# A 7x7 convolution for attention over 49 shifts: rows in polynomial form, column pairs by three products, the input kept on chip

## The chip, the cores and the metric

The kernel runs on one core of a Trainium2 chip. Its engines are TensorE (PE; its weight loads are listed apart as PEld), VectorE (DVE), ScalarE (ACT), GpSimd (POOL) and SyncE (SP). Each works through its own queue in order and waits on semaphores; SP's queue, and here and there ScalarE's, issue the DMA transfers. Everything is fp32. The metric is device time in microseconds (us), lower is better.

## The reference

Two layers, on x of shape (4, 256, 64, 64). Layer 0 makes 49 weights for every pixel and adds up 49 shifted copies of x with them. Layer 1 is a bottleneck block whose three normalisations use the batch's own statistics.

```python
# layer 0
k = conv(x, w1, pad=6, rhs_dilation=2) + b1        # w1: (128, 256, 7, 7)
k = conv(k, w2) + b2                               # w2: (49, 128, 1, 1)
attn = softmax(k, axis=1)                          # over the 49
shifts = stack([xp[:, :, 2*u:2*u+64, 2*v:2*v+64] for u in range(7) for v in range(7)], axis=1)
x = einsum('bkchw,bkhw->bchw', shifts, attn)       # xp: x padded by 6
# layer 1
h = relu(bn(conv(x, w1, 1x1)))                     # 256 -> 64
h = relu(bn(conv(h, w2, 3x3, pad=1)))              # 64 -> 64
out = relu(bn(conv(h, w3, 1x1)) + x)               # 64 -> 256
```

## The kernel before

No nonlinear step lies between the first two convolutions, so the kernel multiplies w1 by w2 first (`product`, line 332) and runs one 7x7 convolution from 256 channels to 49 values. As taps are two apart, rows and columns of different parity never meet: an image falls apart into four of 32 x 32, and pixels are ordered by column, image, parities and row tile.

**Rows.** Four output rows of a column need ten input rows. They are computed by evaluating at ten points: 0, infinity, and plus and minus 0.4, 0.8, 1.25 and 2.5. `product` evaluates the weights there. VectorE evaluates x: `combine` makes sums over rows by chains of `scalar_tensor_tensor` (line 150), `mix` makes the values at +p and -p from the even and odd parts, and `apply_factor` divides a factor out of the stored rows between passes. A pass is one pair of points.

**Columns.** `column_convs` (line 262) takes one column of 128 channels x 128 pixels as the stationary operand, in two halves of 64 (`HALVES`), and streams the weights of its 7 column taps, up to 7 x 49 = 343 columns, into PSUM banks that hold strips of eight output columns. Each matmul of the code shows as two records in the profile. There are 32 columns, ten points and two halves of the 256 channels.

**Order.** All five passes run for channel half 0 first. After each strip ScalarE copies the sums out of PSUM and sends them to DRAM (`put_aside`). Meanwhile half 1 of x is sorted into `stage` and kept in DRAM (`ready`, `fsort`). Then the passes run again for half 1: `put_back` brings the sums to PSUM, and `outputs` adds each pass, scaled, into the logits of four rows. Up to there TensorE's and VectorE's order is the program's (`manual_schedule`); in the second half only SP's first part is fixed and a planner orders the rest.

**Behind it.** For a strip of eight columns `exponents` subtracts the maximum (VectorE) and takes Exp (ScalarE); `shares` divides by the sum and writes the 49 weights into one of three padded rows (`pads`). `turn` transposes a half strip with 8 transposes for each of four output rows (line 568), and ScalarE, or ScalarE and VectorE where it is called with `shared`, copies the result into `amat` (lines 575, 573). `gather` (line 768) multiplies x by `amat`: that is the sum over the 49 shifts. The bottleneck follows (lines 801 to 1091).

The lines that matter here:

```python
for s in range(2 * h, 2 * h + 2):                  # L493, passes 1 to 4, half 0
    column_convs(s, u, True)
    put_aside(n, s)
...
if p is None and 0 < s < NS - 1:                   # L660, last pass, half 1
    if s == 2:
        turn(0, 0)
    exponents(s - 1)
    shares(s - 1)
```

Of the kernel before, what the change touches and what calls it, by code (L numbers as in the profile page):

```python
# [64 lines left out]
PIECES = ((0, 16), (16, 24), (40, 24))  # L65
READY = ((0, 1), (1, 4), (4, NT))
HALVES = (slice(0, 64), slice(64, 128))
ROWS2 = 16
NS, WS = 4, 8
KV = K7 * K  # L70
# [5 lines left out]
NR = 19  # L76
CW = 16
RW = R * CW
AT = 2 * (R // 4) * 4 * 2 * 64 * 4
XI = 2 * R * B * Q * NR  # L80
UT = XI + 2 * R * B * Q * NT
ARENA = UT + NH * (2 + 2 * NP) * KV
SW = WS * CW


def _poly(squares):

    c = [1.0]
    for s in squares:
        c = [(c[i - 1] if i else 0.0) - s * (c[i] if i < len(c) else 0.0) for i in range(len(c) + 1)]  # L90
    return c
# [3 lines left out]
def conv_seq_kernel(ctx: ExitStack, tc: tile.TileContext, xp, xt, w1, b1, w2t, b2, m1t, g1, be1,  # L95
                    m2t, g2, be2, m3t, g3, be3, z, mask, pavg, out, ydram):
    nc = tc.nc
    def pool(stack, name, bufs, space=None, **kw):
        if space is not None:
            kw["space"] = space  # L100
        return stack.enter_context(tc.tile_pool(name=name, bufs=bufs, **kw))


    keep = pool(ctx, "keep", 1)
    st1 = keep.tile([P, 2 * NT, 6], F32, name="st1")


# [18 lines left out]


    ready = nc.dram_tensor("ready_dram", (P, NS, 2, SW, NT), F32, kind="Internal").ap()
    fsort = nc.dram_tensor("fsort_dram", (P, 2, 2, RW // 2, NR), F32, kind="Internal").ap()
    aside = nc.dram_tensor("aside_dram", (1 + len(PAIRS), 2, NS, P, WS * K), F32, kind="Internal").ap()  # L130


    arena = pool(ctx, "arenap", 1).tile([P, ARENA], F32, name="arena")
    slots = arena[:, :XI].rearrange("p (k x i) -> p k x i", k=2, i=NR)
    xi = arena[:, XI:UT].rearrange("p (k x t) -> p k x t", k=2, t=NT)

    ut = arena[:, UT:].rearrange("p (h n v) -> p h n v", h=NH, v=KV)

    amat = arena[:, :AT].rearrange("p (g x c m e) -> p g x c m e", g=2, x=R // 2, c=2, e=4)
    XT = NT * C  # L140
    xts = {}

    units = [(b + 2 * g, 2 * a + c) for b in range(2) for g in range(2) for c in range(2) for a in range(2)]

    cst = pool(ctx, "cst", 1)
    w2sb = cst.tile([P, K], F32, name="w2sb")
    b1sb = cst.tile([P, 1], F32, name="b1sb")
    bias = cst.tile([P, K], F32, name="bias")
# [3 lines left out]
    def zero_rows(t):  # L152

        for k, i0, i1 in ((0, 0, 2), (1, 0, 1), (0, NR - 1, NR), (1, NR - 2, NR)):
            nc.gpsimd.memset(t[:, k, :, i0:i1], 0.0)

    zero_rows(slots)

    def sort_x(raw, b, r0, n, dst, w0, last=None, first=None):

        d = dst.rearrange("p k (w b e) i -> p k w b e i", b=B, e=Q)
        nw = d.shape[2]
        for k in range(2):
            m = r0 // 2 + (r0 // 2 + 3 + k) % 2
            count = ((r0 + n) // 2 - m + 1) // 2
            i = (m + 3) // 2
            for a in range(2):
                lo = 2 * m + a - r0
                (last if last and k + a == 2 else first if first and k + a == 0 else nc.scalar.copy)(  # L169
                    d[:, k, :, PLACE[b], 2 * a : 2 * a + 2, i : i + count],  # L170
                    raw[:, lo : lo + 4 * count - 3 : 4, PAD + 2 * w0 : PAD + 2 * w0 + 2 * nw].rearrange(
                        "p r (w c) -> p w c r", c=2
                    ),
                )

    squares = [p * p for p in PAIRS]
    d_zero = 1.0
    for s in squares:
        d_zero *= -s

    passes = [
        (PAIRS[0], None, squares),
        (PAIRS[1], squares[0], squares[1:]),
        (PAIRS[2], squares[1], squares[2:]),
        (PAIRS[3], None, squares[2:]),
        (None, None, squares[2:]),
    ]

    def combine(dst, row, first, coef):

        n = len(coef) - 1
        acc = row(first + 2 * n)
        for i in range(n - 1, -1, -1):
            stt(dst, row(first + 2 * i), coef[i], acc)
            acc = dst

    def even(p, left, row, x0):
        combine(x0, row, 2, _poly([q for q in left if q != p * p]))

    def odd(p, left, row, x1):  # L200
        combine(x1, row, 1, _poly([q for q in left if q != p * p]))

    def mix(p, x0, x1):
        stt(x0, x1, p, x0)
        stt(x1, x1, -2.0 * p, x0)

    def transform(p, left, row, x0, x1):
        if p is None:
            combine(x0, row, 0, _poly(left))
            combine(x1, row, 1, _poly(left))  # L210
            return
        even(p, left, row, x0)
        odd(p, left, row, x1)
        mix(p, x0, x1)

    def rows_of(t, cols=slice(None), tiles=(0, NT)):


        def row(n):
            i = n // 2 + 2 * tiles[0]  # L220
            return t[:, n % 2, cols, i : i + 2 * (tiles[1] - tiles[0]) - 1 : 2]

        return row

    def apply_factor(t, factor, n, cols=slice(None), parities=range(2)):

        for k in parities:
            v = t[:, k, cols, :n]
            stt(v, v, -factor, t[:, k, cols, 1 : n + 1])

    def visit(t, cols, p, left):

        transform(p, left, rows_of(t, cols), xi[:, 0, cols], xi[:, 1, cols])

    def strip(s, n=1):
        return slice(SW * s, SW * (s + n))

    def weights(n, half):

        return (ut[:, half, 1 + n, :], ut[:, half, 1 + NP + n, :]) if n < NP else (ut[:, half, 0, :], ut[:, half, 1 + 2 * NP, :])  # L240

    s_acc = ExitStack()
    accall = pool(s_acc, "accp", 1, PSUM).tile([P, 2 * NS, 512], F32, name="acc")
    acc = [[accall[:, 2 * s + i] for s in range(NS)] for i in range(2)]

    def strip_taps(s, w):

        return max(0, WS * s - w + 3), min(K7, WS * s + WS - w + 3)

    def column_convs(s, u, first):  # L250

        for d in (s - 1, s, s + 1):
            if not 0 <= d < NS:
                continue
            for i in range(2):
                for w in range(WS * s, WS * s + WS):
                    lo, hi = strip_taps(d, w)
                    if lo >= hi:
                        continue
                    o = (w - 3 + lo - WS * d) * K  # L260
                    for part in HALVES:
                        nc.tensor.matmul(  # L262
                            acc[i][d][part, o : o + (hi - lo) * K],
                            xi[:, i, CW * w : CW * w + CW, :].rearrange("p x t -> p (x t)")[:, part],
                            u[i][:, lo * K : hi * K],
                            start=(first and w == max(0, WS * d - 3)),
# [8 lines left out]
    with ExitStack() as s1:  # L275
# [13 lines left out]
        with ExitStack() as s2:  # L289
# [13 lines left out]
            for i, p in enumerate(PAIRS):  # L303
                nc.gpsimd.memset(points[:, i : i + 1], p)
# [844 lines left out]
```

## Time and profile before

| | |
|---|---|
| three runs | 775.61, 776.87 (median), 781.44 us |
| span of the profiled execution | 774.0 us |
| TensorE busy | 698.9 us, 7428 matmul records |
| VectorE busy | 580.0 us, 681 instructions |
| ScalarE, GpSimd busy | 305.2, 93.4 us |
| line 262 (column products) | 4000 records, 365.0 us |
| line 150 on `arena` (row points) | 192 instructions, 296.0 us |
| mean granted TensorE clock | 0.968 |
| DMA | 150.68 MB, mean 195 GB/s |

A run's time holds the span, from the first to the last instruction, and a little around it. Busy time is the union of an engine's instructions; matmuls are pipelined, so a record's duration is longer than its share of the stream. The granted clock is the part of full speed that TensorE was given. In lists, "out<-in" are tiles by their names in the code, "x80" counts instructions, and "<-" names what ended the idle time before.

### The profile page before, as it was taken

To read this page: it belongs to the slowest core of one execution; us is meant where nothing else is said; L and a number is where in the kernel's file an instruction comes from. 1 tells how busy PE (TensorE), PEld (TensorE's weight loads), DVE (VectorE), ACT (ScalarE), POOL (GpSimd) and SP (SyncE) were. 2 spreads that over 40 slices of the span, in tenths; PEclk is the share of its full clock that TensorE was granted. 3 is DMA by queue.
4 is the path that set the end of the run, shared out by engine and by line. 5 is a ranking of instruction groups with operands and counts; after the bars stand their busy time and mean duration, and the time that the engine had idled before them with its cause. 6 is when DMAs were issued, how large, how long until landed. Compare 5 with 4: busy or idle time off the path is not lost.

```text
span 774.0 us, 17422 instructions
## 1 busy us (share of the span) xinstructions
PE 698.9 (90%) x7428; PEld 506.4 (65%) x7428; DVE 580.0 (75%) x681; ACT 305.2 (39%) x600; POOL 93.4 (12%) x171
## 2 busy tenths in 40 slices
PE   1949898999998987999999999999989988998996
PEld 1937776666766654667666678988778863436642
DVE  5899899999839989999999967222232247854797
ACT  4517465112641011111112258433343346346497
POOL 3516100001000020000002213222212201000000
PEclk9979999999999998999999999999999998997997
DMA  8831299713998895111111013566676659144299
GB/s 348 341 161 43 71 323 344 302 42 138 311 351 320 316 378 174 53 43 44 43 42 33 3 58 105 188 237 226 219 233 232 231 188 406 36 156 174 102 391 377
DMA packets 59839, 150.68 MB, mean 195 GB/s; under 512 B 7410, under 2 KB 35698, under 8 KB 56178
## 3 DMA queue, kind: packets, MB, share of 16 engines
q1 hardware_dynamic: 53712, 141.51, 50.7%
q10 hardware_dynamic: 6050, 8.06, 2.9%
q8 instruction: 58, 0.95, 0.5%
q14 instruction: 19, 0.16, 0.1%
HBM read 93.81 MB, written 55.74 MB: 193 GB/s over the span
## 4 chain that ended last, share of the span: by engine, by line
PE 42%; DVE 33%; DMA 10%; issue 6%; ACT 6%; SPq 1%; ACTq 0%; POOL 0%; DVEq 0%
DVE arena L150 20%; PE acc L262 14%; PE acc L768 12%; DMA raw<-in_xp_dram 6%; PE pconv L975 4%; DVE arena L1084 3%; PE acc L801 3%; PE pdirect L963 3%; DVE stage_x L150 3%; PE acc L568 2%; DMA fsort_dram<-stage 2%; DVE outer L150 2%; PE moments L1045 1%; PE pturn L1040 1%; ACT arena L575 1%
## 5 line engine op out<-in xcount | busy, mean ns | idle before, releaser
L262 PE MATMUL acc<-arena 128*64 128x196 f32 (+6 forms) x4000 | 365.0, 345 | 27.4 <-DVE arena L150 13.2
L262 PEld LDWEIGHTS acc<-arena 128*64 128x64 f32 x4000 | 255.3, 138 | 136.3 <-issue 26.8
L150 DVE SCALAR_TENSOR_TENSOR arena<-arena 128x1024 f32<-128x1024 f32 (+7 forms) x192 | 296.0, 1585 | 9.5 <-ACT arena L169 3.6
L768 PE MATMUL acc<-arena,outer 128*64 128x128 f32 x2048 | 115.2, 273 | 9.0 <-issue 6.9
L768 PEld LDWEIGHTS acc<-arena,outer 128*64 128x64 f32 x2048 | 112.7, 137 | 14.5 <-issue 12.7
L809 DVE BATCH_NORM_STATS2 st<-acc 128x6 f32<-128x512 f32 x16 | 11.1, 694 | 68.8 <-PE acc L801 68.8
L122 ACT COPY outer<-outer 64x2048 f32<-64x2048 f32 x15 | 28.5, 1899 | 76.9 <-DMA outer<-in_xt_dram 76.9
L169 ACT COPY stage<-raw 128x128 f32<-128x128 f32 x128 | 44.6, 419 | 28.6 <-DMA raw<-in_xp_dram 23.8
L609 ACT COPY acc<-bks 128x392 f32<-128x392 f32 x40 | 18.6, 488 | 81.2 <-DVE outer L594 53.2
L286 ACT COPY sv<-acc 128x392 f32<-128x392 f32 x40 | 19.2, 485 | 75.2 <-PE acc L262 57.3
L1026 PE MATMUL pconv<-arena,w3m 64*128 64x512 f32 (+1 forms) x144 | 43.4, 591 | 0.6 <-DVE arena L1084 0.6
L150 DVE SCALAR_TENSOR_TENSOR outer<-outer 128x784 f32<-128x784 f32 (+2 forms) x47 | 36.9, 844 | 4.0 <-POOL outer L930 4.0
L123 POOL COPY outer<-outer 64x1792 f32<-64x1792 f32 x15 | 25.1, 1676 | 91.3 <-DMA outer<-in_xt_dram 91.3
L1026 PEld LDWEIGHTS pconv<-arena,w3m 64*128 64x128 f32 x144 | 20.9, 186 | 21.9 <-DVE arena L1084 16.1
L1089 ACT ACTIVATE outer<-arena 128x512 f32<-128x512 f32 (+1 forms) x58 | 34.6, 694 | 1.1 <-DVE arena L865 1.1
L1084 DVE SCALAR_TENSOR_TENSOR arena<-pconv,arena 128x512 f32<-128x512 f32 (+1 forms) x58 | 34.3, 670 | 0.0
L575 ACT COPY arena<-acc 128x512 f32<-128x512 f32 x52 | 27.1, 708 | 14.8 <-PE acc L568 14.4
L169 POOL COPY arena<-raw 128x192 f32<-128x192 f32 (+2 forms) x24 | 27.2, 1158 | 38.6 <-DVE arena L150 32.6
L975 PE MATMUL pconv<-outer,arena 128*128 128x512 f32 x72 | 31.1, 592 | 0.0
L592 ACT COPY outer<-acc 128x784 f32<-128x784 f32 x8 | 6.5, 813 | 59.7 <-PE acc L262 59.7
L789 DVE COPY bks<-acc 128x256 f32<-128x256 f32 x32 | 11.3, 418 | 24.8 <-PE acc L768 24.8
L169 ACT COPY arena<-raw 128x192 f32<-128x192 f32 (+2 forms) x36 | 20.6, 648 | 22.0 <-DVE arena L150 21.0
(149 smaller groups left out, 668.4 us busy)
## 6 DMA issues: line engine op xcount, KB each, us to landing
raw<-in_xp_dram SPq DMA_DIRECT2D x36, 608.0 KB, 5.5
outer<-in_xt_dram SPq DMA_DIRECT2D x17, 896.0 KB, 6.7
out_dram<-outer SPq DMA_DIRECT2D x14, 1024.0 KB, 4.5
arena<-y_dram SPq DMA_DIRECT2D x25, 512.0 KB, 8.2
fsort_dram<-stage SPq DMA_DIRECT2D x2, 4864.0 KB, 15.3
arena<-fsort_dram SPq DMA_DIRECT2D x8, 1216.0 KB, 8.4
y_dram<-outer SPq DMA_DIRECT2D x16, 512.0 KB, 4.6
aside_dram<-sv ACTq DMA_DIRECT2D x40, 196.0 KB, 5.5
```

The source lines that it names most:

```text
L122: nc.scalar.copy(t[:MID], x[MID:])
L123: nc.gpsimd.tensor_copy(t[MID:, : NT - 1], x[:MID, 1:])
L150: nc.vector.scalar_tensor_tensor(out, in0, scalar, in1, ALU.mult, ALU.add)
L169: (last if last and k + a == 2 else first if first and k + a == 0 else nc.scalar.copy)(d[:, k, :, PLACE[b], 2 * a : 2 * a + 2, i : i + count],
L262: nc.tensor.matmul(acc[i][d][part, o : o + (hi - lo) * K], xi[:, i, CW * w : CW * w + CW, :].rearrange("p x t -> p (x t)")[:, part], u[i][ ...
L575: nc.scalar.copy(dst, src)
L768: nc.tensor.matmul(dst[part, :: NT - 1] if edge else pts[c][part, o : o + 128], x[:, i, half * P + part.start : half * P + part.stop], ama ...
L801: nc.tensor.matmul(pt[a * MID : (a + 1) * MID, :], w1m[:, n, :], ys[a, n][:, 512 * i : 512 * i + 512], start=(n == 0), stop=(n == NH - 1), ...
L975: nc.tensor.matmul(m[k], wu[:, k, j, :], vs[k][:, g, j : j + R, :], start=(j == 0), stop=(j == 1))
L1026: nc.tensor.matmul(pt[:, :n], w3m[part, half * P : (half + 1) * P], h2[part, slot, q, lo : lo + n], start=True, stop=True)
L1084: nc.vector.scalar_tensor_tensor(v, conv3(b, q, i, half, lo, n), sc3[:, half : half + 1], v, ALU.mult, ALU.add)
L1089: nc.scalar.activation(dst, v.rearrange("p (r w) -> p r w", w=R), AF.Relu, bias=sh3[:, half : half + 1])
```

## The change

The row transform is turned round. x is sorted once into four planes, the rows 0 to 3 of each tile of four, for all 256 channels, and stays on chip. The four rows are the coefficients of a polynomial of degree 3, so its values at +p and -p take two sums and two mixing instructions (`even_part`, `odd_part`, `mix_plus`, `mix_minus`). The product of that polynomial with the weights' polynomial has ten coefficients; overlapping neighbours are added. Both steps, from points to rows and between tiles, are matmuls with 128 x 128 matrices made on the host (`_mats`, `final`).

Columns go in pairs, even and odd. Three streams replace two times seven taps: even columns with the 4 even taps, odd columns with the 3 odd taps, and their sums (`add_columns`) with the summed taps (4). `join_streams` subtracts the first two from the third and adds what belongs together.

Both channel halves of a pass now run one after the other into the same PSUM banks, so nothing is put aside; weights at the points are kept in DRAM (`wts`) and loaded pass by pass. A pass has two chunks of eight column pairs (c = 0, 1), a chunk four pieces (two halves of channels, two groups of four pairs). The pass for the points 0 and infinity is split: channel half 0 first, before half 1 has been read, with its sums kept in DRAM (`early`), half 1 last. All five engines follow the program's order.

```diff
-    def visit(t, cols, p, left):
-        transform(p, left, rows_of(t, cols), xi[:, 0, cols], xi[:, 1, cols])
...
-    def column_convs(s, u, first):
...
-        def put_aside(n, s):
...
-        def stage_rows(h):
...
-    def outputs(n, p, g):
...
-    def put_back(n, d):
...
+    def load_weights(n, half, slot):
+        w = wbuf[slot]
+        i = slice(0, 2 + 2 * NP, 1 + 2 * NP) if n == ZERO else slice(1 + n, 2 + n + NP, NP)
+        nc.sync.dma_start(out=w[:, :, :TAPS], in_=wts[half, :, i])
+        nc.gpsimd.tensor_tensor(w[:, :, 7 * K : 10 * K], w[:, :, : 3 * K], w[:, :, 4 * K : 7 * K], ALU.add)
+        nc.gpsimd.tensor_copy(w[:, :, 10 * K :], w[:, :, 3 * K : 4 * K])
...
+    def sort_x():
+        raw, half, b, r0 = queued.pop(0)
...
+        by = (nc.scalar.copy, nc.vector.tensor_copy, nc.gpsimd.tensor_copy)
+        for k, who in enumerate((0, 1, 2, 0, 1, 2, 0, 1)):
...
+    def even_part(m, cols):
...
+        nc.vector.scalar_tensor_tensor(main_of(m)[:, 0], x[:, SLOT[2]], p * p, x[:, SLOT[0]], ALU.mult, ALU.add)
...
+    def add_columns(q):
+        v = planes(q)
+        for i in range(2):
+            nc.vector.tensor_tensor(sums_of(q)[:, i], v[:, i, :, 0], v[:, i, :, 1], ALU.add)
+
+    def bank(cn, k):
+        return accall[:, (6 * cn + k) % 8]
...
+    def conv_group(q, st, i):
...
+        for k in range(4):
+            a = a0 + k
+            lo, hi = max(a, base), min(a + (4, 3, 4)[st] - 1, top)
+            x = sums_of(q)[:, i, k] if st == 2 else planes(q)[:, i, k, st]
+            for part in HALVES:
+                nc.tensor.matmul(
+                    pt[part, (lo - base) * K : (hi + 1 - base) * K],
+                    x[:, part],
+                    w[:, (lo - a) * K : (hi + 1 - a) * K],
...
+    def take_plus(cn, st):
...
+        nc.vector.tensor_tensor(s, pt, d, ALU.add)
+        nc.vector.tensor_tensor(d, pt, d, ALU.subtract)
+
+    def join_streams(cn):
...
+        nc.vector.tensor_tensor(t[:, :, :z], t[:, :, :z], t[:, :, 10 * K : 10 * K + z], ALU.subtract)
+        nc.vector.tensor_tensor(t[:, :, : 9 * K], t[:, :, : 9 * K], t[:, :, 20 * K :], ALU.subtract)
+        nc.vector.tensor_tensor(t[:, :, 11 * K : 20 * K], t[:, :, 11 * K : 20 * K], t[:, :, 20 * K :], ALU.add)
...
+        if last:
+            nc.vector.tensor_tensor(t[:, :, :CA], t[:, :, :CA], helds[c], ALU.add)
...
+    def final(task, pt, add=True):
...
+            nc.tensor.matmul(
+                pt[half, o : o + z], mats[:, r, half], ca, start=(one is None), stop=True, skip_group_check=True
+            )
...
+            nc.vector.tensor_tensor(dst, pt[:, :z], dst, ALU.add)
...
+    def run(tasks, cn, count, first=4, banks=2):
+        for _ in range(count):
+            if tasks:
+                n_final[0] += 1
+                final(tasks.pop(0), bank(cn, first + n_final[0] % banks))
...
+        for q, (cn, h, sub) in enumerate(pieces):
...
+            add_columns(q)
+            for do in pending:
+                do()
+            pending = []
+            if make:
...
+                even_part(m, cols)
+                odd_part(m, cols)
...
+                if len(halves) == 2 and in_chunk in (1, 2):
+                    share = len(waiting) if in_chunk == 2 else (len(waiting) + 1) // 2
+                    counts = {g: share * g // 5 - share * (g - 1) // 5 for g in range(1, 6)}
...
+            for g in range(6):
+                conv_group(q, g // 2, g % 2)
+                if make and g == 1:
+                    mix_plus(m)
+                if make and g == 3:
+                    mix_minus(m)
+                if g in counts:
+                    run(waiting, cn - 1, counts[g])
+                if ends and g in (1, 3):
+                    take_minus(cn, g // 2)
+                    take_plus(cn, g // 2)
+            if ends:
+                take_minus(cn, 2)
+                pending += [lambda cn=cn: take_plus(cn, 2), lambda cn=cn: join_streams(cn)]
...
+            if is_last and c == 1 and in_chunk == 1:
+                exponents(0)
+                shares(0)
+        cn = len(chunks) - 1
+        turn(0, 0)
+        turn(0, 1)
+        for do in pending:
+            do()
+        waiting = finals(cn)
+        for s in range(1, NS):
+            run(waiting, cn, 4, 6, 8)
+            exponents(s)
+            if s == 1:
+                shares(1)
...
-        turn(0, 1)
         zero_edges(0)
-        load_xt(xtiles[0], *units[0])
-        exponents(2)
         turn(1, 0)
-        exponents(3)
-        shares(2)
         turn(1, 1)
         zero_edges(1)
+        load_xt(xtiles[0], *units[0])
+        shares(2)
         turn(2, 0)
+        turn(2, 1, True)
+        zero_edges(2)
         shares(3)
         load_xt(xtiles[1], *units[0], 1)
-        turn(2, 1, True)
-        zero_edges(2)
         turn(3, 0, True)
         turn(3, 1, True)
         zero_edges(3)
```

A piece is made ready two pieces ahead (m = q - 2 in the count of the pair passes): its values at +p and -p lie in one of three buffers (`mains`). The column sums have one buffer. The finals of a chunk run in the second and third piece of the next; two PSUM banks are left to them.

## The prediction

> **What bounds the kernel now.** I read the page's busy times and slices first, then the groups by shape, then stages in the timeline.
>
> ```profile
> PE 698.9 (90%) x7428; PEld 506.4 (65%) x7428; DVE 580.0 (75%) x681; ACT 305.2 (39%) x600; POOL 93.4 (12%) x171
> ...
> PE   1949898999998987999999999999989988998996
> ...
> DVE  5899899999839989999999967222232247854797
> ```
>
> Up to slice 24 (some 460 us) TensorE and VectorE are both full; that is the 7x7 stage. Behind it TensorE alone is full, and the change leaves that part's code alone. Two rows fix the stage and the tail behind it:
>
> ```profile
> 48.53 19.83 PE L262 MATMUL acc<-arena 128*64 128x196 f32 x200 [11.13 <-DVE arena L349]
> ...
> 450.90 5.67 PE L262 MATMUL acc<-arena 128*64 128x343 f32 x46
> ...
> 468.28 10.03 ACT L575 COPY arena<-acc 128x512 f32<-128x512 f32 x20
> ...
> 484.75 15.50 PE L768 MATMUL acc<-arena,outer 128*64 128x128 f32 x280
> ```
>
> Column products run from 48.5 to 456.6 (408.1 us); the gather of layer 0 starts at 484.8, 28.2 us later. I forecast the new time of that gather; what follows it (774.0 - 484.8 = 289.2 us) stays.
>
> **TensorE, by columns streamed.** The dense stretch of the old products, each engine's busy time:
>
> ```profile
> 380.00:440.00 60.00, 60.00 (x676) 40.59 (x674) 1.00 0.09 25
> ```
>
> By shape these 676 records stream 141,022 columns in 60 us: 0.4255 ns a column. Each fp32 matmul of the code shows as two records. The old products stream 640x1078 + 480x294 = 831,040 columns: 353.6 us. The new ones: 11 tap blocks of 49 for a column pair instead of 14; 16 pairs give 176 blocks, of which 8 fall off the edges; 168 x 49 x 2 column halves x 2 records x 20 (ten points, two channel halves) = 658,560 columns, 280.2 us, or 7.0 us for each of 40 pieces. New are the 128x128 matrices (`final`): 1,568 columns x 4 rows x 2 x 2 x 5 passes = 125,440, 53.4 us. So TensorE sheds only 20 us of 354.
>
> One rule reads this otherwise. The Trainium skill, "Trainium Kernel Development and Optimization", Best Practices, judges TensorE by MFU and LDWEIGHTS busy share, not by matmul busy time. Weight loads go from 4,000 to 3,840 + 560, so by the load share the line-262 loads of 255.3 us would become 281, a loss of 26 us in place of the gain of 20. Here loads are busy 40.59 of 60 us while columns pass without a gap, so I go by columns.
>
> **VectorE.** Rows for its price:
>
> ```profile
> L150 DVE SCALAR_TENSOR_TENSOR arena<-arena 128x1024 f32<-128x1024 f32 x80 | 95.5, 1248 | 2.3 <-DMA arena<-ready_dram 2.0
> ...
> L593 DVE TENSOR_TENSOR outer<-acc,outer 128x784 f32<-128x784 f32 x8 | 7.8, 976 | 1.0 <-PE acc L262 1.0
> ...
> L349 DVE TENSOR_TENSOR arena<-arena,acc 128x196 f32<-128x196 f32 x14 | 5.0, 359 | 0.5
> ```
>
> 95.5/80 = 1.19 us for 1024 elements. Between 196 and 784 the slope is 1.05 ns an element; back to back four 784s take 3.54 us, so a queued instruction costs about 0.065 us + 1.046 ns an element, PSUM operand or not. Per piece: two column sums of 512 at 0.60, four instructions of 1024 at 1.19: 6.0 us. Per chunk of four pieces: `take_plus` 6 x 0.56 = 3.4; `join_streams` 3.3 (c = 0) or 4.0 (c = 1); adding the finals 3.2 (c = 0) or 4.7 (c = 1). A pass of two chunks: 48 + 22 = 70 us. TensorE's pass: 56 + 10.7 = 66.7. By the busier engine alone four passes would take 281 us.
>
> **They do not overlap that well.** Both queues are in order, and three things tie them: the single buffer of column sums (a piece's sums wait until the last group of the piece before is through), the take-outs, and the finals, which have two banks. Within a piece VectorE does sums, leftovers of the chunk before, even, odd, `mix_plus`, and only then the adds that free a final's bank. The third final therefore stands in TensorE's queue, with the next product groups behind it, until VectorE is through. For a chunk c = 0 (12 finals of the chunk before), from TensorE's end of one third piece to the next: last add 0.8; block of piece four 6.0 + four takes 2.3; block of piece one 6.0 + take 1.2 + join 4.0; in piece two sums, even, odd, mix 4.8 and an add 0.4: 25.5 us. TensorE has had 7.0 + 7.0 + four groups and two finals, 5.0, and idles 6 us. Then third and fourth final, two groups, two long finals 4.4; third piece with six finals 7.0 + 4.0, and 0.4 of bank wait: together 41.3 us. For c = 1 (8 finals): 0.8 + 8.3 + 10.5 + 5.2 = 24.8, then 2.3 and 9.2: 36.3, with some 3.4 us idle. A pass: 77.6 us.
>
> Long idle stretches cost clock. Columns: stretch, PE, PEld, DVE, ACT, POOL busy, granted clock, DMA share, GB/s.
>
> ```profile
> 276.00:278.00 2.00, 0.00 (x0) 0.00 (x0) 0.05 (x1) 0.00 (x0) 1.27 (x1) 1.00 1.05 282
> 278.00:280.00 2.00, 0.98 (x22) 0.94 (x24) 1.97 (x2) 0.98 (x2) 2.00 (x1) 1.00 0.84 343
> ...
> 292.00:294.00 2.00, 0.00 (x0) 0.00 (x0) 2.00 (x4) 0.00 (x0) 0.00 (x0) 1.00 0.99 377
> 294.00:296.00 2.00, 0.00 (x0) 0.00 (x0) 2.00 (x3) 0.00 (x0) 0.00 (x0) 0.66 0.31 84
> 296.00:298.00 2.00, 1.86 (x18) 1.67 (x20) 2.00 (x3) 0.00 (x0) 0.00 (x0) 0.50 0.06 4
> 298.00:300.00 2.00, 2.00 (x14) 1.14 (x12) 2.00 (x3) 0.00 (x0) 0.00 (x0) 0.50 0.13 29
> ```
>
> The 3.0 us gap at 276 left the clock at 1.00; the 5.4 us gap before 296.1 was followed by some 4.4 us of work at 0.50, 2.2 us lost. So the 6 us gap of each later c = 0 chunk costs 2.2 us more (43.5); the 3.4 us gap of c = 1 stands between the two rows, and I let it cost nothing.
>
> **The start.** Now all w1 is read ahead of x, and all of half 0 must be sorted before the first product. With a full queue reads ran at 400 to 440 GB/s:
>
> ```profile
> 12.00:14.00 2.00, 1.19 (x4) 1.00 (x4) 1.90 (x2) 0.76 (x3) 0.00 (x0) 1.00 1.02 433
> ```
>
> At 420: w1 6.42 MB 15.3 us; half 0 of x 8 x 1.245 MB 23.7; the store of weights half 0 (1.76 MB) 4.2; with 2 us to begin, 45.5. Its sorting ends near 48. The weights of the first pass stand behind three more x loads (8.9) and beside the second store (4.2): first product at about 60.4, 11.9 later than now. ScalarE, VectorE and GpSimd share the sorts, three, three and two copies each load, 2 us beside a load's 3 us; they stay hidden.
>
> GpSimd's adding of tap blocks (294 elements) isn't in the trace; its copies of 192 took 1.26 us, so 0.6 to 2 us. It and the loads of weights and matrices (0.35 and 0.26 MB; small loads landed in 2.3 to 13.6 us) are asked for one to two pieces ahead (7 to 14 us), on SP's queue, where nothing else then waits. I count them at nothing; without that cover some 3 us a pass.
>
> **The stage.** Four early pieces: 28 + 2.2 cold + 1.6 waiting on VectorE (which sorts half 1) = 31.8. First pair chunk, no finals: 34.8, set by VectorE (24 + 4.6 left over from the early chunk + 2.3 takes + some 4 by which the sorts have put it behind). Then 36.3, and three times 43.5 + 36.3. The last four pieces have no row work: TensorE 28 + 10.7, waits for two joins 5, clock 1: 45. Sum 60.4 + 31.8 + 34.8 + 36.3 + 239.4 + 45 = 447.7: 9 us before the old 456.6. All DRAM round trips (aside, ready, fsort) vanish; most were hidden; the gaps of 3.0 and 5.4 us above go with them and are in the old 408.
>
> **The tail turns round the gain.** In the old kernel strips 0 and 1 were exponentiated and divided under products. Now only strip 0's logits are complete when the products end. In VectorE's order: last adds 1.8; exponents 0 at 3.7 (the four 784-element instructions of a strip); shares 0 4.6 (two reduces, reciprocals, eight 196s) = 10.1; take, join, held part 6.7 = 16.8; four adds 0.9, exponents 1 3.7, the wait for Exp 0.9, shares 1 4.6 = 26.9; four adds 1.9 and exponents 2 3.7 = 32.5; again for strip 3 and its Exp 0.9 = 39.0. ScalarE's copies for the turn of strip 1 are queued behind that last Exp: three turns at 4.03 (8 copies; 20 took 10.03) = 51.1; the shared turn (64 records of transposes for two took 7.2) 3.6 = 54.7; shares 3, moved behind it, half 2.3, two shared turns 7.2 = 64.2. Its load of the second x tile waits for shares 3 too; I count it as hidden by the last turns but for 1 us, in place of up to 5 if it isn't. Tail 65 against 28.2: 37 us lost.
>
> **Sum.** 447.7 + 65 = 512.7 against 484.8: +28, span 802. The runs' median of 776.87 stands 2.9 above the span of 774.0: 805.
>
> **Bounds.** Start: 56 if weights pass the x loads, 68 at 365 GB/s: -4, +8. Clock: no gap pays -9, c = 1 gaps pay too +9. VectorE rows 2% off: 6 either way. Tail: turns of strip 1 beginning earlier -10, the x tile late +4. Taken together, not all at once: 786 to 824.
>
> **Rivals.**
> - *The engines overlap after all.* Place: the third final in the second piece. If VectorE reaches its adds before TensorE needs the bank, passes fall from 79 to the 70 of VectorE's plain sum, 66.7 at best: 3.5 passes x 9 to 13 = 31 to 45 less: 760 to 774, say 767. It decides from 71 us a pass, 8 us (a tenth) below my chain. For it: both sums lie under 71. Against: the block of piece one is 11.2 us beside TensorE's 7.0, and nothing runs ahead of the single sums buffer.
> - *The clock stays down.* Gaps of 3.4 us pay too, and the start is late: 805 + 9 + 8 = 822, up to 832. The trace has a 3.4 us gap at 78.6 followed by 0.50.
> - *The short products buy nothing.* If the pieces' short groups (49 to 196 columns) don't stream at 0.4255 ns, TensorE gains no 20 us; but it is not the later engine in most blocks: +5, inside the range.
>
> **Chances.** Forecast 0.6, overlap 0.2, clock and start 0.12, something between (a shorter tail, 770 to 785) 0.08. The range 766 to 826 reaches into both rivals. Runs of the old kernel spread 0.75%, so 1% is what can be told from no change: faster 0.18, same 0.10, slower 0.72.
>
> **What will show it.** The chain should name VectorE's `arena` instructions and the tail's ScalarE copies; TensorE's products should take some 280 us with idle time ahead of finals, released by VectorE; the first product at 60, the last at 448, the gather at 513; the clock at 0.5 after the c = 0 gaps. Wrong if products idle less than 20 us in all, or the tail is under 50.

## The result, and the profile after

| | before | changed |
|---|---|---|
| median of six runs each | 776.37 us | 834.96 us |
| lowest to highest | 775.42 to 781.44 | 832.53 to 842.61 |
| span of the profiled execution | 774.0 | 840.8 |
| first column product | 48.5 | 68.5 |
| last column product | 456.6 | 473.8 |
| gather of layer 0 starts | 484.8 | 546.1 |
| DMA | 150.68 MB | 108.73 MB |

The changed kernel is slower: 1.0754 times the time before, 95% interval 1.0705 to 1.0803. The profiled execution of the changed kernel happens to be the longest of its six (842.61 us, mean granted clock 0.914; the others 0.919 to 0.931), so some 8 us of its span belong to that execution. Where that matters, marks of the experiments that share its code stand beside it.

The page of the changed kernel answers the rows shown of before: busy times, slices, the chain that ended last by engine, and the groups of column products (L336), finals (L409), adds of finals (L418) and column sums (L317).

```profile
PE 708.5 (84%) x7828; PEld 578.3 (69%) x7828; DVE 549.6 (65%) x863; ACT 237.5 (28%) x431; POOL 98.0 (12%) x187
...
PE   3947989796989798879898685899998897997996
...
DVE  1562999897889797979565577723332224883697
...
PEclk9977989898999898979999895899999998997997
...
PE 46%; DVE 38%; DMA 8%; ACT 4%; issue 3%; POOL 1%; SPq 0%; ACTq 0%; DVEq 0%; POOLq 0%
...
L336 PE MATMUL acc<-arena 128*64 128x196 f32 (+2 forms) x3840 | 314.4, 321 | 25.0 <-DMA arena<-wts_dram 16.6
...
L409 PE MATMUL acc<-arena,late 128*64 128x294 f32 (+2 forms) x400 | 71.9, 447 | 16.8 <-DVE arena L418 10.0
L418 DVE TENSOR_TENSOR arena<-acc,arena 128x392 f32<-128x392 f32 (+3 forms) x80 | 37.4, 482 | 56.0 <-PE acc L409 52.8
L317 DVE TENSOR_TENSOR arena<-arena 128x512 f32<-128x512 f32 x80 | 54.0, 714 | 16.4 <-PE acc L336 16.4
```

Three readings. VectorE is busy for 65% of the span and TensorE for 84%, both below what they were, as shares; the chain changes between the two all the time. TensorE's finals wait for VectorE's adds, and those adds wait 52.8 us for TensorE's finals: each queue waits for the other. And the clock row has 7s and 8s all through the stage, where the kernel before had 9 nearly everywhere:

```profile
PEclk9979999999999998999999999999999998997997
```

### The profile page after: what moved, and what is told of

It is laid out like the page before. It is cut to its first block, busy times and chain, and to the rows that moved or that the text cites. A ratio compares the mean times of both kernels' runs of the same rounds, so it can differ in the third digit from the quotient of the medians.

```text
span 840.8 us, 18024 instructions
## 1 busy us (share of the span) xinstructions
PE 708.5 (84%) x7828; PEld 578.3 (69%) x7828; DVE 549.6 (65%) x863; ACT 237.5 (28%) x431; POOL 98.0 (12%) x187
## 2 busy tenths in 40 slices
DMA packets 45106, 108.73 MB, mean 129 GB/s; under 512 B 5603, under 2 KB 26211, under 8 KB 40419
## 4 chain that ended last, share of the span: by engine, by line
PE 46%; DVE 38%; DMA 8%; ACT 4%; issue 3%; POOL 1%; SPq 0%; ACTq 0%; DVEq 0%; POOLq 0%
PE acc L336 12%; PE acc L724 9%; PE acc L409 5%; DVE arena L317 5%; DVE arena L1040 4%; DVE arena L296 4%; DVE arena L291 4%; DVE arena L285 4%; PE pconv L931 4%; PE acc L475 4%; PE acc L757 3%; DMA arena<-in_xt_dram 3%; PE pdirect L919 3%; PE acc L195 3%; DVE arena L301 3%
## 5 line engine op out<-in xcount | busy, mean ns | idle before, releaser
L336 PE MATMUL acc<-arena 128*64 128x196 f32 (+2 forms) x3840 | 314.4, 321 | 25.0 <-DMA arena<-wts_dram 16.6
L336 PEld LDWEIGHTS acc<-arena 128*64 128x64 f32 x3840 | 283.3, 142 | 62.1 <-issue 27.0
L724 PE MATMUL acc<-arena 128*64 128x128 f32 x2048 | 117.7, 277 | 10.7 <-issue 10.3
L724 PEld LDWEIGHTS acc<-arena 128*64 128x64 f32 x2048 | 115.2, 139 | 16.1 <-issue 15.2
L409 PE MATMUL acc<-arena,late 128*64 128x294 f32 (+2 forms) x400 | 71.9, 447 | 16.8 <-DVE arena L418 10.0
L418 DVE TENSOR_TENSOR arena<-acc,arena 128x392 f32<-128x392 f32 (+3 forms) x80 | 37.4, 482 | 56.0 <-PE acc L409 52.8
L317 DVE TENSOR_TENSOR arena<-arena 128x512 f32<-128x512 f32 x80 | 54.0, 714 | 16.4 <-PE acc L336 16.4
L475 PE MATMUL acc<-late,arena 128*128 128x128 f32 x256 | 38.2, 319 | 25.4 <-DVE arena L418 13.1
L409 PEld LDWEIGHTS acc<-arena,late 128*64 128x64 f32 x400 | 29.5, 149 | 24.6 <-DVE arena L418 11.1
L982 PE MATMUL pconv<-arena,late 64*128 64x512 f32 (+1 forms) x144 | 43.4, 590 | 0.6 <-DVE arena L1040 0.6
L1045 ACT ACTIVATE arena<-arena 128x512 f32<-128x512 f32 (+1 forms) x72 | 43.4, 717 | 1.3 <-DVE arena L821 1.1
L296 DVE SCALAR_TENSOR_TENSOR arena<-arena 128x1024 f32<-128x1024 f32 x32 | 39.5, 1235 | 1.1
L301 DVE SCALAR_TENSOR_TENSOR arena<-arena 128x1024 f32<-128x1024 f32 x32 | 39.4, 1230 | 0.4
L291 DVE SCALAR_TENSOR_TENSOR arena<-arena 128x1024 f32<-128x1024 f32 x32 | 39.0, 1219 | 0.0
L285 DVE SCALAR_TENSOR_TENSOR arena<-arena 128x1024 f32<-128x1024 f32 x32 | 39.0, 1219 | 0.0
```

The costliest lines, as they stand in the source:

```text
L285: nc.vector.scalar_tensor_tensor(main_of(m)[:, 0], x[:, SLOT[2]], p * p, x[:, SLOT[0]], ALU.mult, ALU.add)
L291: nc.vector.scalar_tensor_tensor(main_of(m)[:, 1], x[:, SLOT[3]], p * p, x[:, SLOT[1]], ALU.mult, ALU.add)
L296: nc.vector.scalar_tensor_tensor(t[:, 0], t[:, 1], p, t[:, 0], ALU.mult, ALU.add)
L301: nc.vector.scalar_tensor_tensor(t[:, 1], t[:, 1], -2.0 * p, t[:, 0], ALU.mult, ALU.add)
L317: nc.vector.tensor_tensor(sums_of(q)[:, i], v[:, i, :, 0], v[:, i, :, 1], ALU.add)
L336: nc.tensor.matmul(pt[part, (lo - base) * K : (hi + 1 - base) * K], x[:, part], w[:, (lo - a) * K : (hi + 1 - a) * K], start=(h == halves[ ...
```

## The experiments

All start from the changed kernel. Marks in us from each run's own profile; a piece is one of the 40 groups of column products, piece 8 begins the second chunk of the first pair pass. Gains are differences of medians from the changed kernel's 834.96; ratios are to the kernel before, run beside each experiment (medians 775.62 to 777.87). A mark moves by some us between executions of the same code: the first product came at 64.3 to 68.5 us in the runs of the table that leave the start alone.

| run | median | first product | piece 8 | last product | gather less last product |
|---|---|---|---|---|---|
| changed | 834.96 | 68.5 | 136.9 | 473.8 | 72.4 |
| e_start | 829.57 | 51.7 | 132.7 | 467.3 | 69.6 |
| e_start2 | 831.59 | 50.7 | 132.3 | 462.2 | 69.6 |
| e_start3 | 819.28 | 50.5 | 123.1 | 454.5 | 69.6 |
| e_warm2 | 817.64 | 68.1 | 136.1 | 456.1 | 69.4 |
| e_pool | 837.42 | 67.8 | 134.1 | 473.9 | 69.7 |
| e_order | 794.21 | 67.3 | 136.3 | 430.0 | 69.6 |
| e_exps | 836.03 | 67.9 | 135.6 | 469.4 | 70.5 |
| e_tail | 831.86 | 68.3 | 137.5 | 471.9 | 65.7 |
| e_tail2 | 826.29 | 64.3 | 133.7 | 469.7 | 58.7 |
| combo1 | 780.09 | 50.4 | 131.4 | 425.7 | 60.3 |
| combo2 | 765.85 | 50.7 | 121.9 | 416.4 | 56.6 |

### The clock in the waits

```diff
+                if g == 3 + c and counts and in_chunk == 1 and n != ZERO:
+                    for _ in range((5, 2)[c]):
+                        idle_group(q, 0, 0)     # 8 matmuls, stationary operand all zero, start=False, stop=False
                 if g in counts:
                     run(waiting, cn - 1, counts[g])
```

> Matmuls with a stationary operand of zeros are put into TensorE's queue ahead of the third final of the second piece of a chunk (five groups of 8, some 6.7 us, for c = 0; two, some 2.7 us, for c = 1): they add zero and nothing is left out. My theory: the waits themselves stay, but TensorE isn't idle in them, and the 20 us or so that products lose at half clock behind the eight waits go: granted clock of the stage above 0.97, 818 to 826 us. Rival: the time lost at half clock lies beside VectorE's work anyway, the wait alone counts: 832 to 842.

> The run with matmuls of zeros once more, with the block of zeros in columns of its own (in the first run its first four columns lay over the last weights, so that those matmuls added something there); nothing is left out. My theory: as before, 815 to 822 us, clock of the stage above 0.97. Rival: 830 or more.

Measured: 818.91 and 817.64 us, the second 1.0502 times before (1.045 to 1.0554). In the first run the block of zeros lay partly over the last weights, so that its matmuls added something there; in the second they add zero, and the second is the one that counts. Matmuls that add nothing make the kernel 17 us faster. The changed kernel around the third final of piece 13, by the busy times of a stretch (stretch, its length, busy us and instructions of PE, PEld, DVE, ACT, POOL, granted clock, DMA share, GB/s):

```profile
188.00:194.00 6.00, 0.74 (x12) 0.46 (x8) 5.93 (x7) 0.00 (x0) 0.00 (x0) 0.99 0.00 0
194.00:196.00 2.00, 0.43 (x6) 0.43 (x8) 1.97 (x5) 0.00 (x0) 0.00 (x0) 0.50 0.00 0
196.00:198.00 2.00, 2.00 (x18) 1.58 (x16) 1.08 (x2) 0.00 (x0) 0.00 (x0) 0.50 0.00 0
198.00:200.00 2.00, 2.00 (x21) 1.66 (x19) 0.31 (x1) 0.00 (x0) 0.00 (x0) 0.50 0.00 0
```

The same place in e_warm2:

```profile
188.00:190.00 2.00, 2.00 (x28) 2.00 (x26) 2.00 (x3) 0.00 (x0) 0.00 (x0) 1.00 0.00 0
190.00:192.00 2.00, 2.00 (x28) 2.00 (x26) 1.97 (x3) 0.00 (x0) 0.00 (x0) 1.00 0.03 8
192.00:194.00 2.00, 1.80 (x28) 1.36 (x26) 2.00 (x5) 0.00 (x0) 0.00 (x0) 1.00 0.00 0
194.00:196.00 2.00, 2.00 (x32) 1.94 (x30) 0.61 (x3) 0.00 (x0) 0.00 (x0) 1.00 0.00 0
```

VectorE works through the wait in both; TensorE comes out of it at half clock in one and at full clock in the other. Adding up busy time times (1 - clock) over the stage in steps of 2 us gives 24.8 us lost in the changed kernel and 6.8 in e_warm2; the difference of 18.0 is close to the 17.3 us by which the stage is shorter (405.3 to 388.0). The changed kernel's figure is the top of a range: six other traces with the same passes lose 19.6 to 23.7. The stage's own rhythm shows it chunk by chunk: c = 0 chunks took 44.9 to 45.7 us and now 42.7 to 42.8, c = 1 chunks 37.4 to 39.1 and now 36.1 to 37.1. The theory holds; the rival is excluded.

When does a wait cost clock? Not by its length alone. In each trace the granted clock changes only at the borders of a fixed grid of steps of 3.41 us. In the changed kernel a gap of 2.04 us that lay inside one step was followed by half clock:

```profile
429.39:432.80 3.41, 1.37 (x30) 1.12 (x27) 2.68 (x3) 0.00 (x0) 1.05 (x1) 1.00 0.00 0
432.80:436.21 3.41, 3.41 (x36) 3.31 (x34) 0.62 (x2) 0.00 (x0) 0.00 (x0) 0.50 0.02 5
```

In e_exps a gap of 3.20 us, from 399.66, that lay across a border was not:

```profile
397.54:400.95 3.41, 1.78 (x20) 1.02 (x16) 3.41 (x5) 0.00 (x0) 0.00 (x0) 1.00 0.01 2
400.95:404.37 3.42, 1.51 (x18) 1.20 (x20) 3.39 (x6) 0.00 (x0) 0.00 (x0) 1.00 0.95 323
404.37:407.78 3.41, 3.41 (x46) 2.80 (x43) 2.04 (x4) 0.00 (x0) 1.58 (x2) 1.00 0.89 373
```

The traces of the changed kernel and of the twelve experiments hold 1,338 whole steps at full clock between the first and the last product. Of 1,241 in which TensorE was idle for less than 2.0 us, one was followed by half clock (1.86 us idle); of 97 in which it was idle for 2.0 us or more, all were.

### The order of the passes

```diff
+    ORDER = {       # what VectorE is given before group 0 and after groups 0 to 5 of a piece, by (c, piece of the chunk)
...
+        (0, 1): ((), ("pend",), ("even",), (), ("odd",), ("plus",), ("minus",)),
...
+    COUNTS = {      # finals of the chunk before, after groups 0 to 5
+        (0, 0): (0, 0, 0, 0, 0, 2), (0, 1): (0, 0, 0, 2, 0, 1), (0, 2): (2, 0, 2, 1, 2, 0),
+        (1, 0): (0, 0, 0, 0, 0, 1), (1, 1): (0, 1, 1, 0, 0, 1), (1, 2): (1, 1, 0, 1, 1, 0),
+    }
...
                 if g in counts:
                     run(waiting, cn - 1, counts[g])
+                rows(g + 1)
```

> Only the order in which the pair passes are written out is changed: the 8 or 12 finals of a chunk are spread over three pieces in place of two, and even, odd, plus and minus of a piece stand behind the adds of finals where these are due, not ahead of them. The same instructions run; nothing is left out. My theory: a pass takes 83.5 us because the two queues stop each other in turn (TensorE idles some 7 us of a c = 0 chunk while VectorE is busy, and VectorE some 8 us afterwards), not because either is full: by VectorE's own 70 us a pass up to 13 us a pass are to be had, and with the waits the half clock goes: 788 to 806 us. Rival: VectorE's work of a pass is what counts, as taking the sums off it in another run brought nothing: 828 or more.

Measured: 794.21 us, 1.0213 (1.0159 to 1.0267): 41 us gained by the order alone. The chain of the changed kernel shows what was wrong with the order written (start, us, what): it runs through VectorE alone for a stretch, then through TensorE alone.

```profile
149.20 1.23 DVE arena L301
150.43 1.20 DVE arena L317 x2
151.63 1.14 DVE arena L285
152.77 1.15 DVE arena L291
153.94 1.23 DVE arena L296
155.59 1.25 PE acc L409 x4
156.84 2.12 PE acc L336 x16
158.96 0.94 PE acc L409 x4
159.90 3.66 PE acc L336 x46
```

Busy times of 170 us of the pair passes, in the changed kernel:

```profile
200.00:370.00 170.00, 148.47 (x1790) 127.78 (x1788) 142.29 (x176) 7.95 (x14) 5.50 (x8) 0.92 0.05 13
```

and in e_order:

```profile
200.00:370.00 170.00, 164.14 (x2108) 155.08 (x2106) 165.79 (x206) 10.31 (x18) 16.03 (x9) 0.98 0.07 22
```

VectorE goes from 142.29 to 165.79 of 170 us, TensorE passes 2108 records in place of 1790. A pass takes 71.8 us (39.6 + 32.2) in place of 82.6 to 83.8: VectorE's plain sum of 70 is reached within 3%. TensorE's idle stretches over 1.5 us in the stage add up to 22.1 us in place of 42.3, and the time lost to the clock falls from 24.8 to 10.0, so that up to 15 of the 41 us are clock. What remains bounds the stage by VectorE's work.

### Column sums on GpSimd

```diff
-            nc.vector.tensor_tensor(sums_of(q)[:, i], v[:, i, :, 0], v[:, i, :, 1], ALU.add)
+            who = nc.gpsimd if NE <= q < NE + n_pair else nc.vector
+            who.tensor_tensor(sums_of(q)[:, i], v[:, i, :, 0], v[:, i, :, 1], ALU.add)
...
```

> The column sums of the 32 pieces of pairs move from VectorE to GpSimd (two of 512 elements a piece, some 1.5 us each by its 294-element row of 0.865 us); the adding of the tap blocks is issued later on GpSimd so that nothing there waits for a load; nothing is left out. My theory: in-order queues tie TensorE to VectorE, so taking 1.2 us a piece off VectorE's blocks shortens each wait by 2 to 4 us and brings some back under the length that costs clock: 7 to 10 us a pass, 800 to 808 us. Rival: the sums on GpSimd come later than TensorE asks for them, or the two engines slow each other: 830 to 845.

Measured: 837.42 us, 1.0781 (1.0724 to 1.0839): nothing gained; my number failed and the rival's 830 to 845 holds. The cause is on the page of e_pool: GpSimd's sums, and VectorE's `odd_part`, which took 1219 ns in the changed kernel.

```profile
L326 POOL TENSOR_TENSOR arena<-arena 128x512 f32<-128x512 f32 x64 | 99.6, 1567 | 197.0 <-PE acc L345 183.6
...
L299 DVE SCALAR_TENSOR_TENSOR arena<-arena 128x1024 f32<-128x1024 f32 x32 | 49.6, 1550 | 0.0
```

Instructions of VectorE that lie beside a sum on GpSimd are stretched, single ones from 1.22 to 2.30 us, and most of what was taken off is paid back: VectorE was busy 240.0 us of the 28 pieces from piece 8 on in the changed kernel and 235.0 here. So VectorE's queue was nearly as long as before, and the run says nothing against the coupling. One meeting of the two (start, us):

```profile
230.33 3.80 POOL L326 TENSOR_TENSOR arena<-arena 128x512 f32<-128x512 f32 x2 [4.52 <-PE acc L345]
230.69 2.30 DVE L299 SCALAR_TENSOR_TENSOR arena<-arena 128x1024 f32<-128x1024 f32 x1
233.03 2.18 DVE L304 SCALAR_TENSOR_TENSOR arena<-arena 128x1024 f32<-128x1024 f32 x1
```

By the single records GpSimd's first sum ends at 231.91, VectorE's `odd_part` 1.08 us later, GpSimd's second sum 1.13 us after that, and `mix_plus` (L304) 1.08 us after that: each ends about one instruction's work after the other engine's. The Trainium skill, "SBUF — State Buffer", section "SBUF: two separate sides", says that VectorE and GpSimd share one pair of ports under an exclusive lock when VectorE reads two SBUF operands and GpSimd reads SBUF; the stretched rows are of that kind. By that rule the one that comes second is held until the other has ended, and these records agree with it.

### The start

The first run copies the first pass's weights on chip:

```diff
                 if (half, v) == (0, 6):
                     keep_weights(0)
+                    nc.scalar.copy(wbuf[1][:, :, :TAPS], uts[0][:, :: 1 + 2 * NP])
+                    add_taps(wbuf[1])
...
-        load_weights(ZERO, 0, 1)
```

> The first pass's weights of half 0 are copied on chip by ScalarE (686 elements) in place of the trip through DRAM; nothing is left out. My theory: the first product waits for that trip, 11.84 us by the profile, which stands behind the reads of x; half 0 is sorted at 55.5 us. First product at 56 to 58 in place of 68.5, and all of it is kept: 823 to 825 us. Rival: the start is bound by the reading of x itself, and what comes earlier is lost again where half 1 of x is waited for: 831 us or more.

Measured: 829.57 us, 1.067 (1.0613 to 1.0728). The first product comes at 51.7, 16.8 us earlier: the wait was the trip, and all of it. In the changed kernel's waits (engine, tile, line <- releaser: us, times, longest) it stands as

```profile
PE acc L336 <- DMA arena<-wts_dram: 16.6, 1, 16.6
```

But piece 8 is only 4.2 us earlier. In the waits of e_start from 40 to 125 us:

```profile
PE acc L340 <- DVE arena L321: 15.4, 5, 5.9
DVE arena L246 <- DMA arena<-in_xp_dram: 15.4, 3, 10.0
```

VectorE's queue holds sorts of half 1 that wait for reads of x (L246), ahead of the sums that TensorE needs (L321). The rival was right for most of the gain. The second run takes VectorE out of those sorts:

```diff
-        for k, who in enumerate((0, 1, 2, 0, 1, 2, 0, 1)):
+        for k, who in enumerate((0, 2) * 4 if half else (0, 1, 2, 0, 1, 2, 0, 1)):
...
+        copy = nc.vector.tensor_copy if chunks[cn][3] else nc.scalar.copy
+        copy(sides(cn)[:, 1, o : o + z], bank(cn, 2 * st + 1)[:, :z])
```

> As the run with the first weights copied on chip, and VectorE is kept free of half 1's sorting: ScalarE and GpSimd sort it, four copies each, and VectorE takes the early sums out in place of ScalarE; nothing is left out. My theory: in the first run of the start 17 us were gained ahead of the first product and 8 lost again, because VectorE's queue holds sorts that wait up to 10 us for a read of x ahead of the column sums that TensorE needs; without them piece 6, the first that needs half 1, starts at 100 to 108 in place of 118 (122.8 in the changed kernel): 812 to 820 us. Rival: half 1 of x cannot be on chip much earlier, whoever sorts it: 826 or more.

Measured: 831.59 us, 1.0686 (1.0614 to 1.0759); piece 8 at 132.3: a miss. Waits of e_start2 from 50 to 125 us:

```profile
POOL arena L226 <- DMA arena<-wts_dram: 13.1, 1, 13.1
...
DVE arena L355 <- DMA early_dram<-arena: 7.8, 1, 7.8
```

GpSimd, which now has half of these sorts, stands 13.1 us before the adding of tap blocks for the next weights, ahead of the sorts, so raw buffers stay full, reads of x stop, and the store of the early sums behind them on SP's queue comes late. The third run issues that adding two pieces later and takes one more copy of each sort off GpSimd:

```diff
-        load_weights(0, 0, 0)
+        load_weights(0, 0, 0, True)     # without its add_taps
...
+            if early_part and q == 2:
+                add_taps(wbuf[0])
...
-        for k, who in enumerate((0, 2) * 4 if half else (0, 1, 2, 0, 1, 2, 0, 1)):
+        for k, who in enumerate((0, 0, 2, 0, 0, 2, 0, 2) if half else (0, 1, 2, 0, 1, 2, 0, 1)):
```

> As the second run of the start, with two edits: GpSimd's adding of tap blocks for the first pair pass is issued two pieces later, and ScalarE takes five, GpSimd three of the eight copies of a sort of half 1; nothing is left out. My theory: in that run GpSimd stood 13 us on the weights' trip through DRAM, ahead of the sorts that free the three raw buffers, so the reads of x stopped, and the store of the early sums, behind them on SP's queue, held VectorE's take-outs 6.5 us; without that the second pair chunk (piece 8) starts at 115 to 123 us in place of 132: 815 to 824 us. Rival: VectorE and GpSimd slow each other in the early pieces (row instructions of 1.22 us took up to 1.65 there), and that sets the pace: piece 8 at 129 or later, 828 or more.

Measured: 819.28 us, 1.0511 (1.0447 to 1.0576); piece 8 at 123.1, at the far end of the 115 to 123 I gave. The start was a chain of three waits, each the next one's cover: only with the third gone did most of the first one's 17 us show, 13.8 us at piece 8 and 15.7 in the median. Which of the last two edits brought how much was not separated.

### The tail

```diff
-            nc.scalar.activation(e, e, AF.Exp)
+        for h in range(2):
+            nc.scalar.activation(columns(s, h), columns(s, h), AF.Exp)
```

> Only this: the maxima and subtractions of both halves of a strip stand ahead of both Exp; nothing is left out. My theory: the reduce of the second half waits 0.95 us for the Exp of the first in each of four strips, a wait of the written order and not of the data, and the whole chain of the tail waits with it: tail 3 to 4 us shorter than the 69.7 of the other runs that leave the tail alone, 830 to 833 us. Rival: ScalarE's queue gives it back, since the second Exp comes as late as before: no more than 1 us.

Measured: 836.03 us, 1.0744 (1.0688 to 1.0799), tail 70.5: the rival was right. VectorE's waits in the tail of the changed kernel (L434 is the reduce of `exponents`, L443 that of `shares`, L436 the Exp):

```profile
DVE arena L480 <- ACT arena L482: 5.6, 7, 2.9
DVE mx L434 <- ACT arena L436: 4.2, 4, 1.3
DVE sm L443 <- ACT arena L436: 3.8, 3, 1.8
```

and of e_exps, whose lines stand one lower:

```profile
DVE sm L444 <- ACT arena L437: 7.7, 3, 3.8
...
DVE arena L418 <- ACT arena L437: 1.8, 1, 1.8
```

The 4.2 us before the maxima are gone, and the wait before the sums grows by 3.9: my reading is that two Exp of 0.86 us in a row stand between VectorE's two halves wherever they are put, as long as `shares` follows soon. Two further runs therefore put other work between:

```diff
+            if q == last:
+                exponents(0)
...
+        run(waiting, cn, 4, 6, 8)
+        exponents(1)
+        run(waiting, cn, 4, 6, 8)
+        shares(1)
+        run(waiting, cn, 4, 6, 8)
+        turn(1, 0)
+        exponents(2)
+        turn(1, 1)
+        exponents(3)
```

> Only the order of the tail is changed; nothing is left out. All eight finals of the last-but-one chunk run in piece 38, exponents of strip 0 stand beside the last products, the maxima and subtractions of both halves of a strip stand ahead of both Exp, the shares of strip 1 and its turns stand ahead of the exponents of strips 2 and 3. My theory: the tail of 72.4 us is a serial order and not work; VectorE has some 40 us of it left and ScalarE some 39 that lie beside each other: tail 46 to 52, time 808 to 815. Rival: ScalarE's copies for the turns set the tail whatever the order: 828 or more.

> As the run with the tail's order changed, and further: exponents of strip 2 ahead of the shares of strip 1, shares of strip 2 ahead of the exponents of strip 3, so that no reduce waits behind an Exp that stands behind copies of a turn (4.2, 2.0 and some 5 us of VectorE idle in that run); nothing is left out. My theory: tail 55 to 59 in place of 65.7, 820 to 826 us. Rival: the copies out of PSUM set the pace: 830 or more.

Measured: e_tail 831.86 us, 1.0709 (1.0655 to 1.0763), tail 65.7; e_tail2 826.29, 1.0618 (1.0544 to 1.0691), tail 58.7. The first fell far short of the 46 to 52 I gave: among others the reduce of strip 3 waited 3.2 us for the Exp of strip 2, which stood behind eight copies of `turn(1, 0)`. The second, with that order mended, hit its 55 to 59. So the tail is order for some 11 us of 69.6; the rest I did not get out of it. Why a reduce waits for an Exp on other columns of the same tile I did not settle.

### All together

> The three edits of this call together (order of the passes, start, tail); nothing is left out. My theory: they touch three stretches that follow each other, so they add: some 20 + 35 + 13 us less than the changed kernel's 835, 757 to 775 us, under the kernel before. Rival: what is gained at the start is lost where the passes wait for half 1 of x, and the stage only moves its waits: 785 or more.

Measured: 780.09 us, 1.0056 (1.0018 to 1.0094): 5 us over my range. Passes and tail brought their parts; the start is that of e_start2, which had not (piece 8 at 131.4).

> Order of the passes as before, the start as in this call, and a further edit of the tail: adds of strip 3 and shares of strip 3 earlier, twelve finals of the last pair chunk spread so that none stands ahead of its join; nothing is left out. My theory: gather starts some 15 to 20 us earlier than in the first combination (485.9): start 8 to 12, last pass 3 to 4, tail 3 to 6: 757 to 768 us, under the kernel before. Rival: the early pieces are bound by VectorE and GpSimd beside each other and only the tail's part comes: 770 to 778.

Measured: 765.85 us, 0.9858 (0.9785 to 0.993): inside the 757 to 768 forecast, 1.4% faster than the kernel before (0.7 to 2.2%) and 69 us faster than the changed kernel, with the same arithmetic in another order. Its page:

```profile
PE 680.3 (89%) x7828; PEld 571.5 (75%) x7828; DVE 544.9 (72%) x842; ACT 245.1 (32%) x445; POOL 116.2 (15%) x195
...
PE   3989789989998999899997759999989979988996
...
DVE  1567999999999999999667986223232337854797
...
PEclk9999899999998999999999979999999998998997
```

VectorE is 94% busy in the pair passes (159.88 of the 170 us from 200 on), the clock drops only three times there (at 164.9, 236.5 and 311.6), and the gather starts at 473.0.

## Why the prediction was half right

The direction and the mechanism came as forecast; the size did not: +28 us forecast, +58.6 measured, 9 us above the range. Three terms of the sum were too small: the clock above all, then the start and the tail. Step by step, with the terms as the prediction put them:

- **TensorE by columns, VectorE by rows: right.** Undisturbed pieces follow each other at 6.5 to 7.3 us, 7.0 forecast; row instructions took 1219 to 1235 ns, 1.19 us forecast back to back. The rule on load share that I weighed (Trainium skill, "Trainium Kernel Development and Optimization", Best Practices) was worked out to 281 us of loads for products and finals together; measured were 283.3 for the products alone and 42.5 for the finals, yet where nothing waits, time goes by the columns.
- **The waits of the two queues: right.** The c = 0 gap was forecast at 6 us and is 6.82; the c = 1 gap at 3.4 and is 3.20. With the clock kept up the chunks take 42.8 and 36.1 us (e_warm2), against the chain's 41.3 and 36.3.
- **The clock: mis-sized, the step that failed most.** I let the c = 1 gap "cost nothing", by one row of before (3.0 us, no drop), and a c = 0 gap 2.2 us. With the cold early pieces and the 1 us of the last four that is 9.8 us; measured were 24.8 (19.6 to 23.7 in the six other traces). This is 15 of the 18 us between the stage's 405.3 and my 387.3. Against e_warm2 the c = 1 chunks lost 1.3 to 2.8 us each, the c = 0 chunks 2.1 to 3.0. The 3.0 us gap of before lay across a border of the 3.41 us steps, 1.57 us on one side and 1.47 on the other; the c = 1 gaps of 3.20 us put 2.2 to 3.0 us into one step all four times in the changed kernel, and 23 of 28 such gaps (3.07 to 3.20 us) in the seven traces with these passes cost clock. In e_order gaps of 2.92 and 2.93 us cost it, one of 2.71 across a border did not. The Trainium skill, "TensorE: Matmul & The Clock Gate", Part 1, tells of windows of activity of some 3.4 us that run freely, which the steps of 3.41 us agree with. Its section "Why this matters for your kernels" warns of gaps over some 3 us; here 2.04 us inside one step cost clock and 3.20 across two did not. So one gap of before was no price for another, and the c = 1 gaps belonged into the sum, not only into the range. The row of the 5.4 us gap was also read short: half clock lasted until 301.45, 5.3 us of work in place of 4.4.
- **The start: mis-sized, in the reading of x.** "Its sorting ends near 48": it ended at 55.5, and from there to the first product it was 13.0 us, 12.4 forecast. I counted the sorts as hidden. But the first sort stood on ScalarE behind the copies of `product` from 22.7, when its x had landed, to 27.6; the fourth read waits for that buffer and was issued at 29.6. The transfers moved 290 GB/s from 22 to 30 us and 378 from 36 to 46, where I had 420. What I missed besides is that piece 6 waits for half 1 of x, so that the first product is not the start's last word (e_start2, e_start3).
- **The tail: order right, waits too short.** Forecast 65, measured 72.4, and 69.4 to 69.7 in six runs with the same code. I counted the wait for Exp twice at 0.9; VectorE waited 4.2 + 3.8 + 1.0 us for it, 7.2 us more.
- **Behind the gather: "289.2 stays".** 294.7 in this execution, 289.9 to 291.1 in those six runs, and 288.2 in combo2: that the changed kernel makes it longer is not shown.
- **The last four pieces:** 45 forecast, 48.1 measured, 46.4 in e_warm2.

Start 8, stage 18, tail 7 and behind 5 make the 39 us by which the profiled span of 840.8 exceeds my 802; in an execution of median length it is some 31.

**The rivals.** "The clock stays down" (822, up to 832, chance 0.12) is what happened, in both of its parts: the start cost the 8 us that I gave it, the clock 10 to 15 in place of 9, and the tail came on top. "The engines overlap after all" did not happen in the kernel as written. Its 31 to 45 us match the 41 that e_order gained, with the pass at 71.8 where I put the point of decision at 71, but this is in part luck: up to 15 of the 41 are clock, which that price did not hold. "The short products buy nothing" fell with the 7 us pieces. The sentence that named what would prove me wrong (idle under 20 us, tail under 50) named the wrong side only.

## What to carry to other kernels

When two engines that run in order are each busy some 85% of a stage, write down where each stands in its queue when the other needs it: here the same instructions took some 83 us a pass in one order and 71.8 in another. A wait of TensorE is not priced by its length alone: here it cost clock behind it when some 2.0 us of idle time fell into one step of 3.41 us, which depends on where in the step the wait begins. Keeping TensorE busy with matmuls of zeros is a quick way to measure that part. A wait that is removed shows its worth only when what stands next in the same queue is looked up; at the start it took three edits, and in the tail one edit moved 4 us from one wait to another.

## What I had not expected of the hardware

- Matmuls that compute nothing made the kernel 17 us faster (e_warm2), by the granted clock alone.
- The clock falls by steps of 3.41 us and by TensorE's idle time within one, so the same 3.20 us wait cost clock in one place and nothing in another.
- GpSimd's additions stretch VectorE's: `odd_part` 1219 to 1550 ns in the mean, up to 2.30 us, and GpSimd's own addition of tap blocks went from 865 to 1347 ns (L218 in e_pool).
